# A graph kernel in which each block multiplies the columns up to its own number less two, in place of a number set per strip of four

## Chip, core and metric

The kernel runs on one NeuronCore of a Trainium2 chip. The metric is the device time of one execution in microseconds (us). Before the change the median of four executions is 3410.36 us (3400.29 to 3419.5). The lines of the profile come from one further execution, taken by the hardware profiler.

The engines are named as the profile names them: PE is TensorE's matrix multiply, PEld its weight load, DVE is VectorE, ACT is ScalarE, POOL is GpSimd and SP is SyncE, which here only issues DMAs. "ACTq" and "SPq" are the issuing of DMAs by ACT and SP. An f32 matmul of the program appears in the profile as two MATMUL rows, each with its weight load.

## What is computed

There are 3327 nodes with 128 features (padded to 3328, 26 blocks of 128) and a sparse adjacency matrix `adj` of 3327 x 3327 floats. Two layers follow each other:

```python
h = relu(layernorm(x))                       # layer 0: GATv2, four heads
s = exp(8 * tanh(leaky_relu(x1[:,None] + x2[None,:]) @ a / 8)) * adj
x = x + concat_heads(leaky_relu((s / s.sum(-1)) @ h @ Wlin.T)) @ w
h = relu(layernorm(x))                       # layer 1: GCN
A_t = adj + I;  D = rowsum(A_t) ** -0.5
x = x + relu((D[:,None] * A_t * D[None,:]) @ (h @ W.T + b))
```

The change is in layer 1's product of the adjacency matrix with the new features: (26 blocks of rows) x (26 blocks of columns), each of 128 x 128. "Column j" below is a block of 128 columns of `adj`, and it needs the finished layer-1 features of block j.

## The kernel before, in words

Layer 0 goes over the 26 blocks of rows, one after the other, some 125 us each in the middle of the kernel. For a block, two halves (`hb`) of nine groups (`m`) run: rows of the non-zero neighbours are gathered from a table in DRAM by indirect DMAs (L595, POOL), turned on PE (L622, result `z`), joined with the block's own features on DVE (L638, result `r`), reduced to scores on PE (L657) and summed with their weights (L706, L724). The order on each engine is written out by hand: the main loop calls `slot()`, some 108 times a block, and each slot steps generators on by one `yield`: the rest of a score (`finish`), the close of a block (`close`), and the preparation of the next block (`prep`).

`close(b)` (L729 to L799) ends a block: among others ACT scales the sums (L740), PE turns and multiplies (L746, L757, L768), DVE adds the residual and stores it (L772, L774), ACT centres it (L779, L780, L785), PE multiplies by layer 1's weights (L792), and ACT writes layer 1's features of the block over `x_sb[:, b]` (L797). From then on the block is "closed", and others may multiply with it.

`prep(b)` runs beside the block b - 1. It loads the rows of `adj`, turns them four columns at a time on PE (L365), copies them to SBUF as `at` on ACT (L367) and stores them to DRAM as `AT_d` (L370, issued by ACT). Here layer 1 begins: `known_step` multiplies the columns that are closed (`x_sb[:, j]`) with the transposes while these are still in SBUF. One call, a group, handles up to four columns: an accumulating matmul for each (L379), then a copy (L383, first group) or an addition on DVE (L385) into `part1`, which SP stores at the end (L387). How many columns a block does so is `finished(b)`: 4 * (b // 4) - 2, so 2 for blocks 4 to 7, 6 for 8 to 11, then 10, 14 and 18, and 22 for blocks 24 and 25. In all this makes 244 matmuls in 72 groups.

All that is left is worked off strip by strip, a strip `s` being four blocks of rows, so a matmul (`x_sb[:, j]` against the stored transposes of four blocks) has 512 columns:

- `begin()`: in the last block and a half, strips 1, 2 and 3 do twelve columns each, from `finished(4 * s)` on. SP brings the transposes two columns at a time (`bring`, L913: `adjb<-AT_d`) into a ring of three; the 36 matmuls are L924, one in every four slots.
- `layer1()`: the end. 74 pairs (s, j) stand in a list `work`, cut into seven pieces of eleven. `strip()` brings a piece with DMAs that are issued in turn by SP and ACT (L898: `g<-AT_d`) into one of the four gather buffers. The matmuls are L988; the first of them are put between the last slots of block 25. At a strip's end `strip_out` adds the parts of before (loaded by `strip_in`, L943 to L947), turns, scales and stores the result (L955 to L968).

`columns()` makes the DMAs of a part: consecutive columns of a strip, up to four, are one DMA for each block of rows. The pieces that matter below are the fifth and sixth: the fifth holds strip 2's columns 24 and 25, strip 3's 22 to 25 and strip 4's 14 to 18; the sixth strip 4's 19 to 25 and strip 5's 18 to 21. The seventh has the rest of strip 5 and strip 6 (blocks 24 and 25). Before the change, the DMAs of the fifth to seventh piece are 16, 12 and 6.

Of the kernel before, what the change touches and what calls it, by code (L numbers as in the profile page):

```python
# [15 lines left out]
P = 128  # L16
# [215 lines left out]
def _sparse_layers(tc, nc, x, adj, w1, w2, a, wlin, w, gw, gb, gb_sb, gwT, x_sb, dinv, flag, ident, out):  # L232
# [15 lines left out]
    NB = NP // P  # L248
# [8 lines left out]
    with ExitStack() as l0:  # L257
# [70 lines left out]
        def bank():  # L328
            return ps_tr.tile([P, 4, P], F32, name="tr").rearrange("p a b -> p (a b)")
# [14 lines left out]

        def finished(b):

            return max(0, 4 * (b // 4) - 2)

        def load(b):
            blks[b].adjb = pa.tile([P, NP], F32, name="adjb")  # L350
# [2 lines left out]
        def prep(b, k):  # L353
# [7 lines left out]
            def tables_step(j0):  # L361
                n = min(4, NB - j0)
                pt = ps_tr.tile([P, 4, P], F32, name="tr")
                for q in range(n):
                    nc.tensor.transpose(pt[:, q, :], adjb[:, (j0 + q) * P:(j0 + q + 1) * P], ident)  # L365
                at = pat.tile([P, 4, P], F32, name="at") if b else blks[0].at[j0 // 4 % 4]
                nc.scalar.copy(at[:, :n, :], pt[:, :n, :])  # L367
                at0 = b * TURN + j0 * P * P
                eng = nc.scalar if b else nc.sync
                eng.dma_start(AT_d[at0:at0 + n * P * P].rearrange("(b p c) -> p b c", p=P, c=P), at[:, :n, :])  # L370
                js = range(min(n, finished(b) - j0))
                if len(js):
                    known.append(known_step(j0, js, at))
# [471 lines left out]
        def allow(kind):  # L845
            state[kind] += 1
# [27 lines left out]
        PAIR = 2  # L874
        BEGUN = 12
        strips = {}
        early = {s: range(finished(4 * s), finished(4 * s) + BEGUN) for s in (1, 2, 3) if finished(4 * s) + BEGUN < NB - 3}

        def columns(v, part):

            at = 0
            while at < len(part):
                s, j = part[at]
                n = 1
                while n < 4 and at + n < len(part) and part[at + n] == (s, j + n):
                    n += 1
                for b in range(4 * s, min(4 * s + 4, NB)):
                    a0 = b * TURN + j * P * P
                    c0 = (b - 4 * s) * P
                    yield v[:, at:at + n, c0:c0 + P], AT_d[a0:a0 + n * P * P].rearrange("(j p i) -> p j i", p=P, i=P)  # L890
                at += n

        def strip(part):
            g = rows_in()
            v = g.rearrange("p t c -> p (t c)")[:, :PIECE * 4 * P].rearrange("p (j i) -> p j i", j=PIECE)
            for k, (to, of) in enumerate(columns(v, part)):
                eng = nc.scalar if k % 2 else nc.sync
                eng.dma_start(to, of)  # L898
            for at, key in enumerate(part):
                strips[key] = v[:, at]  # L900

        def begin():

            work = [(s, j) for s in early for j in early[s]]
            pairs = [work[i:i + PAIR] for i in range(0, len(work), PAIR)]
            if not work:
                return
            thirds = pa.tile([P, NP], F32, name="adjb")[:, :3 * PAIR * BANK].rearrange("p (k j i) -> p k j i", k=3, j=PAIR)

            def bring(k):  # L910
                if k < len(pairs):
                    for to, of in columns(thirds[:, k % 3], pairs[k]):
                        nc.sync.dma_start(to, of)  # L913

            for k in range(3):
                bring(k)
            for _ in range(14):
                yield
            po = None
            for i, (s, j) in enumerate(work):  # L920
                assert blks[j].closed
                if j == early[s][0]:
                    po = bank()
                nc.tensor.matmul(po, x_sb[:, j, :], thirds[:, i // PAIR % 3, i % PAIR], start=(j == early[s][0]), stop=(j == early[s][-1]))  # L924
                if i % PAIR == PAIR - 1:
                    bring(i // PAIR + 3)
                if j == early[s][-1]:
                    part2 = pv.tile([P, H, P], F32, name="outT").rearrange("p h i -> p (h i)")
                    nc.scalar.copy(part2, po)
                    nc.sync.dma_start(part2_d[:, 4 * s * P:4 * s * P + BANK], part2)  # L930
                for _ in range(4):
                    yield

        def first_column(s):
            return early[s][-1] + 1 if s in early else finished(4 * s)

        def strip_in(s):

            n = min(4, NB - 4 * s)
            r0 = pr.tile([P, 2, BANK], F32, name="r0", bufs=3).rearrange("p k (b d) -> p k b d", b=4)[:, :, :n]  # L940
            r1 = pr.tile([P, 2, BANK], F32, name="r1").rearrange("p k (b d) -> p k b d", b=4)[:, :, :n]
            rows = slice(4 * s * P, (4 * s + n) * P)
            nc.sync.dma_start(r0[:, 0], xn_d[rows, :].rearrange("(b p) d -> p b d", p=P))  # L943
            if finished(4 * s):
                nc.sync.dma_start(r1[:, 0], part1_d[:, rows].rearrange("p (b i) -> p b i", b=n))
            if s in early:
                nc.sync.dma_start(r0[:, 1], part2_d[:, rows].rearrange("p (b i) -> p b i", b=n))  # L947
            return n, rows, r0, r1

        def strip_out(s, po, n, rows, r0, r1):  # L950

            ot, t, xo = r0[:, 1], r1[:, 1], r0[:, 0]
            po = po[:, :n * P].rearrange("p (b i) -> p b i", b=n)
            if s in early:
                nc.vector.tensor_add(ot, po, ot)  # L955
            if finished(4 * s):
                nc.vector.tensor_add(ot, ot if s in early else po, r1[:, 0])
            elif s not in early:
                nc.scalar.copy(ot, po)
            yield  # L960
            yield
            pt = ps_tr.tile([P, 4, P], F32, name="tr")
            for k in range(n):
                nc.tensor.transpose(pt[:, k, :], ot[:, k, :], ident)
            nc.vector.tensor_add(t, pt[:, :n, :], x_sb[:, 4 * s:4 * s + n, :])
            nc.vector.tensor_tensor(t, t, dinv[:, 4 * s:4 * s + n, None].to_broadcast([P, n, D]), OP.mult)
            nc.vector.scalar_tensor_tensor(xo, t, 0.0, xo, op0=OP.max, op1=OP.add)
            nc.scalar.dma_start(out[rows, :].rearrange("(b p) d -> p b d", p=P), xo)  # L968
# [8 lines left out]
        def layer1():  # L977
            ending, sums, ins = [], {}, {}
            for i, (s, j) in enumerate(work):
                if i == in_front:  # L980
                    yield "all"
                w = min(4, NB - 4 * s) * P
                if s not in sums:
                    sums[s] = ps_z.tile([P, 2, BANK], F32, name="z")[:, 0]
                if j == min(NB - 1, first_column(s) + 4 * (s not in front)):
                    assert len(ending) < 2
                    ins[s] = strip_in(s)
                nc.tensor.matmul(sums[s][:, :w], x_sb[:, j, :], strips[s, j][:, :w], start=(j == first_column(s)), stop=(j == NB - 1))  # L988
                if i % PIECE == PIECE - 1 or i == len(work) - 1:
                    allow("g")  # L990
                ending[:] = [f for f in ending if next(f, "end") != "end"]
                if j == NB - 1:
                    ending.append(strip_out(s, sums.pop(s), *ins.pop(s)))
                yield "one"
            for e in ending:
                for _ in e:
                    pass
# [194 lines left out]
        with tc.manual_schedule():  # L1192
# [4 lines left out]
            n = len(groups)  # L1197
# [8 lines left out]
            for i in range(-1, n + 1):  # L1206
                if i + 1 < n:
                    slot()
                if 0 <= i < n:
                    b, hb, m = groups[i]  # L1210
                    if (b, hb, m) == (max(0, NB - 2), 1, 0):
                        state["early"] = begin()
                    rs[i] = stage_z(blks[b], hb, m, slot, partial(scores, i - 1))
                elif i == n:
                    scores(i - 1)
            lay = layer1()
            todo = "one"
            while ends or tails or state["early"] is not None:
# [67 lines left out]
def kernel(  # L1286
# [26 lines left out]
    gb_sb = const.tile([P, D], F32, name="gb_sb")  # L1313

    _sparse_layers(tc, nc, x, adj, w1, w2, a, wlin, w, gw, gb, gb_sb, gwT, x_sb, dinv, flag, ident, out)


# [46 lines left out]
```

## Time and profile before

| what | value |
|---|---|
| median of four executions | 3410.36 us (3400.29 to 3419.5) |
| the profiled execution, its own time | 3408.4 us |
| its span, first to last instruction | 3406.7 us |
| mean granted TensorE clock | 0.886 |
| DMA traffic | 826.94 MB, mean 243 GB/s |
| busy: POOL 1711.0 us (50%), ACT 685.0 us (20%) | |
| last slot of block 25 to the end | about 3310 us to 3406.7 us |

The page of the profile gives busy times and shares of the span, a strip of 40 slices, DMA queues, the chain of work that ended last, and the costliest groups of instructions. A group's line names the source line, the engine, the operation, what is written and read, the number of instructions, then its busy time, the mean nanoseconds of one, and the idle time of the engine just before it with what ended most of that. A PE row's duration includes its way through the array, so rows that follow each other overlap; the spacing of starts tells what one of them costs.

### The profile page before, as it was taken

What the parts mean: (1) busy time and instruction counts of PE and PEld (TensorE: products, weight loads), DVE (VectorE), ACT (ScalarE), POOL (GpSimd) and SP (SyncE); (2) the same over time, 40 slices, a digit from 0 to 9 for tenths busy, and PEclk for the clock granted to TensorE, in tenths of its full rate; (3) what the DMA queues carried; (4) which work ended last, traced back from release to release, by engine and by line L of the source; (5) the groups of instructions that cost most, each with busy time, mean ns of one, the idle gap of its engine ahead of it and who ended that gap; (6) DMA issues with size and microseconds to landing.
All of it is one profiled execution on the core that took longest, in us unless ns stands there. A gap on an engine that the chain in (4) does not pass through costs nothing.

```text
span 3406.7 us, 52385 instructions
## 1 busy us (share of the span) xinstructions
PE 2634.4 (77%) x19410; PEld 1840.0 (54%) x19410; DVE 2097.5 (62%) x6426; ACT 685.0 (20%) x1703; POOL 1711.0 (50%) x1822
## 2 busy tenths in 40 slices
PE   6687777877787787787777877777777787777887
PEld 4464555555464565565555555555555565555553
DVE  6676666666666666665665665665665665665442
ACT  3122122212211221221121221221221221121110
POOL 3555555555554545545545555545545445445420
PEclk8789888899988988888988898988898988888999
DMA  9978777777777867867867777777776777777886
GB/s 327 316 258 264 220 250 260 222 253 260 254 237 238 265 213 251 263 199 241 272 204 238 255 227 228 251 229 225 250 241 217 249 235 221 242 217 218 259 256 185
DMA packets 417844, 826.94 MB, mean 243 GB/s; under 512 B 38435, under 2 KB 288815, under 8 KB 414255
## 3 DMA queue, kind: packets, MB, share of 16 engines
q0 software_dynamic: 141440, 619.41, 55.6%
q1 hardware_dynamic: 165343, 147.87, 14.0%
q10 hardware_dynamic: 110800, 56.25, 5.6%
q8 instruction: 156, 2.56, 0.3%
q14 instruction: 105, 0.86, 0.1%
HBM read 754.47 MB, written 113.22 MB: 255 GB/s over the span
## 4 chain that ended last, share of the span: by engine, by line
PE 52%; DVE 17%; issue 12%; another core or an unknown queue 10%; DMA 5%; POOL 2%; ACT 1%; SPq 0%; ACTq 0%; DVEq 0%; POOLq 0%
PE z L622 19%; PE s L657 10%; DVE r L638 9%; PE ag L706 5%; PE z L627 3%; PE tr L675 3%; POOL g L595 2%; DVE cand L422 2%; PE tr L379 2%; PE ag L724 2%; DMA g<-table,idx 1%; DMA g<-AT_d 1%; PE z L988 1%; PE tr L365 1%
## 5 line engine op out<-in xcount | busy, mean ns | idle before, releaser
L595 POOL DMA_INDIRECT g<-table,idx x1664 | 1588.7, 955 | 1363.7 <-PE ag L706 800.2
L638 DVE TENSOR_TENSOR r<-z,x1n 128x1024 f32<-128x1024 f32 x832 | 1011.7, 1216 | 844.2 <-remote 318.8
L622 PE MATMUL z<-ident,g 128*128 128x128 f32 x6656 | 1051.1, 303 | 167.2 <-issue 109.1
L622 PEld LDWEIGHTS z<-ident,g 128*128 128x128 f32 x6656 | 857.0, 157 | 352.5 <-issue 232.4
L657 PE MATMUL s<-r,sel 128*2 128x512 f32 (+1 forms) x3744 | 549.1, 606 | 132.5 <-DVE r L638 82.8
L666 ACT COPY ssb<-s 128x512 f32<-128x512 f32 x260 | 147.1, 566 | 842.2 <-PE s L657 275.8
L706 PE MATMUL ag<-g,wt 128*32 128x133 f32 x3328 | 234.8, 309 | 99.1 <-issue 97.9
L657 PEld LDWEIGHTS s<-r,sel 128*2 128x2 f32 x3744 | 82.6, 84 | 404.4 <-issue 271.3
L675 PE MATMUL tr<-ident,ssb 128*128 128x128 f32 x988 | 172.3, 300 | 105.1 <-issue 97.3
L706 PEld LDWEIGHTS ag<-g,wt 128*32 128x32 f32 x3328 | 134.4, 118 | 219.4 <-issue 210.3
L422 DVE MAX8 cand<-codes 128x8 f32<-128x52 uint16 x1664 | 216.2, 201 | 0.0
L675 PEld LDWEIGHTS tr<-ident,ssb 128*128 128x128 f32 x988 | 129.5, 155 | 131.5 <-issue 115.6
L595 POOL DMA_INDIRECT ge<-table,idxo x104 | 99.1, 953 | 180.5 <-PE ag L724 90.2
L379 PE MATMUL tr<-at,x_sb 128*128 128x128 f32 x488 | 96.4, 353 | 115.3 <-ACT at L367 109.7
L367 ACT COPY at<-tr 128x512 f32<-128x512 f32 (+1 forms) x175 | 97.4, 557 | 416.0 <-remote 199.4
L686 ACT ACTIVATE th<-sc 128x32 f32<-128x32 f32 x260 | 58.8, 226 | 506.5 <-DVE sc L681 235.8
L379 PEld LDWEIGHTS tr<-at,x_sb 128*128 128x128 f32 x488 | 81.0, 249 | 141.7 <-ACT at L367 130.5
L633 DVE TENSOR_TENSOR r<-z,x1n 128x128 f32<-128x128 f32 x104 | 30.2, 290 | 195.4 <-PE z L627 147.0
L365 PE MATMUL tr<-ident,adjb 128*128 128x128 f32 x676 | 123.2, 308 | 33.7 <-DMA adjb<-in_adj_dram 15.6
L627 PE MATMUL z<-oi,x1b 128*128 128x256 f32 x416 | 137.3, 414 | 4.9 <-issue 4.9
L453 DVE MAX8 lists<-cand 128x8 f32<-128x272 f32 (+1 forms) x338 | 133.0, 394 | 2.2
L622 PE MATMUL z<-ident,ge 128*128 128x128 f32 x416 | 89.2, 291 | 45.5 <-issue 33.2
(199 smaller groups left out, 2614.3 us busy)
## 6 DMA issues: line engine op xcount, KB each, us to landing
adjb<-in_adj_dram SPq DMA_DIRECT2D x26, 1664.0 KB
table<-AT_d SPq DMA_DIRECT2D x26, 1664.0 KB
AT_d<-at ACTq DMA_DIRECT2D x150, 256.0 KB
g<-table,idx POOLq DMA_INDIRECT x1664
table<-img SPq DMA_DIRECT2D x12, 1296.0 KB
adjb<-AT_d SPq DMA_DIRECT2D x72, 128.0 KB
g<-AT_d SPq DMA_DIRECT2D x25, 256.0 KB
g<-AT_d ACTq DMA_DIRECT2D x25, 256.0 KB
```

Of the source, the lines that this page charges most:

```text
L365: nc.tensor.transpose(pt[:, q, :], adjb[:, (j0 + q) * P:(j0 + q + 1) * P], ident)
L379: nc.tensor.matmul(pq[:, :P], x_sb[:, j0 + q, :], at[:, q, :], start=(q == 0), stop=(q == js[-1]))
L422: nc.vector.max(cand[:, c, 8:].rearrange("p (r s) -> p r s", s=32)[:, :, sgm % 32], codes.rearrange("p a b -> p (a b)")[:, sgm % 32 * SEG: ...
L453: nc.vector.max(top, of)
L595: return nc.gpsimd.indirect_dma_start(out=g[:, t, lo:hi], out_offset=None, in_=tab, in_offset=bass.IndirectOffsetOnAxis(ap=at[:, t:t + 1], ...
L622: nc.tensor.matmul(z[:, i, q * P:(q + 1) * P], g[:, m % 2 * 4 + q, c0:c0 + D], ident, is_transpose=True, start=(q == 0 or m < 8), stop=(m ...
L627: nc.tensor.matmul(z[:, i, :n], k.x1b[:, h * D:(h + 1) * D], k.oi[:, hb * n:(hb + 1) * n], start=False, stop=True, skip_group_check=True)
L638: nc.vector.tensor_tensor(r.rearrange("p h (i s) -> p h i s", s=16), z.rearrange("p h (i s) -> p h i s", s=16), k.x1n[:, 2 * hp:2 * hp + 2 ...
L657: nc.tensor.matmul(k.s[32 * h:32 * h + 2, :n], sel[:, h, 31 - at:33 - at], r[h // 2][:, h % 2, :n], start=(at == 0), stop=(at == 1 or m == 8))
L666: nc.scalar.copy(ssb[:, :nk * P], s[:, :nk * P])
L675: nc.tensor.transpose(pt[:, q, :], ssb[:, q * P:(q + 1) * P], ident)
L706: nc.tensor.matmul(ag[32 * cg:32 * cg + 32, u, :WORK], wt[:, t].rearrange("p h q -> p (h q)"), g[:, t, f0:f0 + WORK], start=(w == 0 and t ...
```

## The change

`finished(b)` becomes b - 2 for every block from 4 on. So block 5 multiplies three columns beside its transposes, block 6 four, block 7 five, and so on. What begins a strip in `begin()` and `layer1()` is still `finished(4 * s)`, which has the value of before; but a column of which some blocks of the strip already have the product is now brought and multiplied only for the others (`blocks(s, j)` of them), with a narrower matmul. `columns()` joins only columns with the same number of blocks to one DMA.

```diff
         def finished(b):
-            return max(0, 4 * (b // 4) - 2)
+            return b - 2 if b >= 4 else 0
...
+        def blocks(s, j):
+            return sum(finished(b) <= j for b in range(4 * s, min(4 * s + 4, NB)))
...
-                while n < 4 and at + n < len(part) and part[at + n] == (s, j + n):
+                while n < 4 and at + n < len(part) and part[at + n] == (s, j + n) and blocks(s, j + n) == blocks(s, j):
                     n += 1
-                for b in range(4 * s, min(4 * s + 4, NB)):
+                for b in range(4 * s, 4 * s + blocks(s, j)):
...
-                nc.tensor.matmul(po, x_sb[:, j, :], thirds[:, i // PAIR % 3, i % PAIR], start=(j == early[s][0]), stop=(j == early[s][-1]))
+                w = blocks(s, j) * P
+                nc.tensor.matmul(po[:, :w], x_sb[:, j, :], thirds[:, i // PAIR % 3, i % PAIR, :w], start=(j == early[s][0]),
+                                 stop=(j == early[s][-1]), skip_group_check=True)
...
-                w = min(4, NB - 4 * s) * P
+                w = blocks(s, j) * P
...
-                nc.tensor.matmul(sums[s][:, :w], x_sb[:, j, :], strips[s, j][:, :w], start=(j == first_column(s)), stop=(j == NB - 1))
+                nc.tensor.matmul(sums[s][:, :w], x_sb[:, j, :], strips[s, j][:, :w], start=(j == first_column(s)), stop=(j == NB - 1),
+                                 skip_group_check=True)
```

Counted on the two built programs, the change moves this:

| line before | before | after |
|---|---|---|
| L379 matmul of 128 columns | 244 | 275 |
| L385 addition on DVE (a group after a block's first) | 50 | 55 |
| L924 matmuls of 128 / 256 / 384 / 512 columns | 0 / 0 / 0 / 36 | 3 / 3 / 3 / 27 |
| L988 matmuls of 128 / 256 / 384 / 512 columns | 0 / 4 / 0 / 70 | 3 / 5 / 2 / 64 |
| L913 DMAs | 72 | 78 |
| L898 DMAs on SP, and as many on ACT but for one | 45 and 45 | 50 and 49 |

## Prediction

> **What bounds the kernel now.** I began with the totals and the chain of work that ended last. No engine is full: PE 77%, DVE 62%, but half of the chain is PE's own work. I then went to the group that grows, L379 (the products beside the transposes), and asked for its line alone.
>
> ```profile
> span 3406.7 us, 52385 instructions
> PE 2634.4 (77%) x19410; PEld 1840.0 (54%) x19410; DVE 2097.5 (62%) x6426; ACT 685.0 (20%) x1703; POOL 1711.0 (50%) x1822
> ...
> PE 52%; DVE 17%; issue 12%; another core or an unknown queue 10%; DMA 5%; POOL 2%; ACT 1%; SPq 0%; ACTq 0%; DVEq 0%; POOLq 0%
> PE z L622 19%; PE s L657 10%; DVE r L638 9%; PE ag L706 5%; PE z L627 3%; PE tr L675 3%; POOL g L595 2%; DVE cand L422 2%; PE tr L379 2%; PE ag L724 2%; DMA g<-table,idx 1%; DMA g<-AT_d 1%; PE z L988 1%; PE tr L365 1%
> ...
> L379 PE MATMUL tr<-at,x_sb 128*128 128x128 f32 x488 | 96.4, 353 | 115.3 <-ACT at L367 109.7
> ```
>
> To see: L379 is 488 rows for 244 matmuls, 96.4 us of PE, so 0.395 us a matmul; its 115.3 us of idle time before it is more than its work, nearly all waiting for ACT's copy L367 of the transposes. In the trace, 38 of its 72 groups start with under half a microsecond of PE idle, 34 with 1 to 6 us, most near 3; 115.3 / 34 is 3.4 us for such a one.
>
> Whether that work is on the path is told by the kernel itself, since blocks differ in it. ACT's row sum of `adj` (L443) comes once in each preparation; the timeline of ACT has its starts. These are those of blocks 3, 7, 11, 15, 19, 23 and 25:
>
> ```profile
> 315.07 2.96 ACT L443 ACTIVATE adjb<-adjb 128x3328 f32<-128x3328 f32 x1
> ...
> 795.96 2.96 ACT L443 ACTIVATE adjb<-adjb 128x3328 f32<-128x3328 f32 x1
> ...
> 1281.02 2.96 ACT L443 ACTIVATE adjb<-adjb 128x3328 f32<-128x3328 f32 x1
> ...
> 1778.75 2.96 ACT L443 ACTIVATE adjb<-adjb 128x3328 f32<-128x3328 f32 x1
> ...
> 2281.77 2.96 ACT L443 ACTIVATE adjb<-adjb 128x3328 f32<-128x3328 f32 x1
> ...
> 2786.85 2.96 ACT L443 ACTIVATE adjb<-adjb 128x3328 f32<-128x3328 f32 x1
> ...
> 3042.31 2.96 ACT L443 ACTIVATE adjb<-adjb 128x3328 f32<-128x3328 f32 x1
> ```
>
> The first column is the start. Divided by the blocks between them, a block takes 120.2, 121.3, 124.4, 125.8, 126.3 and 127.7 us, with 2, 6, 10, 14, 18 and 22 matmuls in it. Blocks with more of them are longer.
>
> Last, the timeline of ACT in the end, where layer 1's loads are issued (columns: start, duration, what; in brackets the idle time before and what ended it):
>
> ```profile
> 3321.49 18.14 ACTq L898 DMA_DIRECT2D g<-AT_d  x18
> 3339.67 0.63 ACT L740 ACTIVATE agn<-ag,rec 128x128 f32<-128x128 f32 x2 [24.50 <-DMA g<-AT_d]
> ...
> 3345.99 8.00 ACTq L898 DMA_DIRECT2D g<-AT_d  x6
> 3354.10 0.40 ACT L779 ACTIVATE agn<-xn,st 128x128 f32<-128x128 f32 x1 [7.52 <-DMA g<-AT_d]
> ```
>
> To see: the close of block 25 (L740, L779) stands behind loads in ACT's order, and ACT is held by issuing them, 18.14 us and 8.00 us. PE's timeline shows PE idle 6.86 us before L746, which L740 releases, and 0.81 us before L784, which L779 releases. Between those PE is busy.
>
> **The change part by part.** All against the profiled execution's 3408.4 us, 2.0 us under the median of the runs shown.
>
> *1. 31 matmuls more at L379, in 5 more groups.* Blocks with b mod 4 = 1, 2, 3 get one, two, three more in each of the strips of blocks 4 to 23, and block 25 one: 5 x 6 + 1 = 31. A fifth column opens a new group only where b mod 4 = 3: five groups, each with a DVE addition (0.28 us by the line's median), a PSUM buffer and a wait for its copy L367. PE's own work: 31 x 0.395 = 12.2 us. What of it lengthens a block comes from the periods: (127.7 - 120.2) / 20 = 0.375 us a matmul, its share of groups in it, so 31 x 0.375 = 11.6 us. But the periods also drift within equal counts, and the later steps are smaller: from 10 to 22 matmuls (127.7 - 124.4) / 12 = 0.275, so 8.5 us. I take 10 us. Bounds: nothing, if the work fills PE's idle 23%; and 12.2 us plus five long waits of 3.4 us, 29.2 us. A gain is excluded: nothing is taken from these blocks.
>
> *2. 18 block columns less at L924, in the last block and a half.* Twelve PE rows of 512 columns start 0.43 us apart, so a full matmul is 0.86 us and a block's share 0.215 us: 18 x 0.215 = 3.9 us of PE. In the chain between 3150 us and the end L924 has 9.7% of 257 us, 24.9 of the 36 x 0.86 = 31.0 us that it works, or 0.8. So -3.1 us, between 0 and -3.9. Six more DMAs on SP (78 for 72, 1.2 MB less in all) are hidden by the ring: a pair is brought three pairs ahead, some 28 us, and the rows of L913 take about half a microsecond to issue. The SP loads queued behind them (L587, L774) keep their places between the same brings. If the cover went, PE would wait for a pair's landing, as in the chain's pieces `DMA adjb<-AT_d` of 4 to 6 us.
>
> *3. 13 block columns less at L988.* 13 x 0.215 = 2.8 us, at PE's busy stretch from 3354 us on, so -2.8 us.
>
> *4. More DMAs for less data in the end.* The fifth piece has 18 for 16, the sixth 18 for 12, the seventh 7 for 6. Where ACT stood for 18 issues before L740 it now stands for 19, and before L779 for 9 in place of 6. An issue waits for an earlier DMA to land (SP's queue: L898 waited 24.2 us in 22 times on `g<-AT_d`; both share eight completion semaphores, so the n-th issue waits for the n-8th). So the cost goes by bytes that must have landed, at 260 GB/s in this stretch: before L740 two single blocks more, 0.13 MB or 0.5 us. In the sixth piece the last issue waited for the 4th DMA (16 blocks of 64 KB) and now waits for the 10th (16 + 12 + 1 + 1 = 30 blocks): 14 x 64 KB, 3.5 us. PE, which already waits 0.81 us there, waits for all of it, with its later matmuls in order behind L784; DVE's and ACT's next steps of the close too. After the 6.86 us idle the granted clock in 3340 to 3344 us was 0.50 and four L988 rows took 3.42 us, not 1.7; I add half of that difference, 0.8 us. Together +4.8 us; bounds 0 (the loads land early, there being 0.8 MB less) and +11 (every issue at the row's mean, 1.01 + 3 x 1.33 = 5 us, the clock's whole 1.7, and SP's four more issues at 1.1 us ahead of the parts that L955 adds).
>
> Sum: +10 - 3.1 - 2.8 + 4.8 = +8.9 us, 3417.3 us for the profiled execution and 3419 us on the median.
>
> One rule of the Trainium skill speaks against the change more strongly. "TensorE: Matmul & The Clock Gate", section "Back-to-back issue gap", gives for a stream of weight loads and matmuls about 81 ns at 128 columns and 131 ns at 512: a block's column alone then costs 2.5 times its share in a strip of four. The rows here say 0.395 against 0.215 us, 1.8 times. By the page part 1 would be 31 x 2.5 x 0.215 = 16.7 us of PE in place of 12.2 us; I stay with the rows.
>
> **The rivals.**
>
> *A. The new groups stall PE in full (slower).* Each of the five new groups (blocks 7, 11, 15, 19, 23) meets the long wait for L367, 3.4 us, and none of the matmuls finds cover: 12.2 + 17.0 - 3.1 + 2.0 = +28.1 us, 3438 us on the median. It decides (over 0.5%, 17 us) from 1.2 us a new group on, with the matmuls uncovered. For it: 34 of 72 groups have such a wait. Against it: from 2 to 22 matmuls five groups are added too, and a block grows only 7.5 us, not 7.9 + 17.
>
> *B. PE's idle time swallows part 1 (a little faster).* Then parts 2 and 3 remain with 0.5 us of part 4: -5.4 us, 3405 us. For it: PE idles 23%, and the first step, 2 to 6 matmuls, cost only 1.1 us a block. Against it: the later blocks.
>
> *C. The end does not get shorter but longer.* The list of 74 pairs stays, the DMAs become more, and ACT holds the close for part 4's upper bound: 10 - 3.1 - 2.8 + 11 = +15 us, 3426 us. So the change would do the opposite of its name in the end. For it: 24.50 and 7.52 us of ACT behind these loads. Against it: 0.8 MB less to bring.
>
> **How the numbers follow.** Forecast 0.62, A 0.16, B 0.12, C 0.10. A measurement of this kernel can tell about 0.5% from no change: 3393 to 3427 us is the same. The forecast and B lie inside; A lies above; of C a third passes the edge with an unlucky part 1. That gives 0.79 the same, 0.19 slower, and 0.02 faster, since all work that leaves the last 300 us is 6.7 us of PE. The range goes from under B to near A: 3402 to 3436 us.
>
> **What would show it.** L379 with 550 rows and about 108 us busy; periods of the blocks with b mod 4 = 3 up by a microsecond or more, of b mod 4 = 0 unchanged; L740 late by about half a microsecond against block 25's last L724 and L779 by 4 us; PE idle before L784 up from 0.81 to some 4 us; the stretch from L784 to the end shorter by 2.8 us. I am wrong if the periods do not grow, or if the new groups' waits at L367 show more than 3 us each on top of them.

## The result, and the profile after

The changed kernel takes 3421.97 us (median of 52 executions, 3401.57 to 3441.94), the kernel before, run beside it, 3408.84 us (78 executions, 3386.67 to 3426.55). The ratio is 1.0042 with a 95% interval from 1.0032 to 1.0053, so the change costs 14.3 us, between 10.9 and 18.1: clear of no change, and under the half percent. The forecast was 3419 us, +8.9 us.

Single executions scatter by 40 us, three times the effect. The profiled execution of the changed kernel happens to be a short one; its span is that of before to the tenth. So its total says nothing, and only stretches inside it are read, beside the same stretches of other kernels where these were profiled. First its page, totals and L379:

```profile
span 3406.7 us, 52541 instructions
PE 2624.2 (77%) x19472; PEld 1852.7 (54%) x19472; DVE 2099.7 (62%) x6431; ACT 682.4 (20%) x1703; POOL 1710.1 (50%) x1822
...
L379 PE MATMUL tr<-at,x_sb 128*128 128x128 f32 x550 | 112.3, 364 | 116.4 <-ACT at L367 110.9
```

To see: 62 rows more at L379 for the 31 matmuls, 112.3 us busy for 96.4. The idle time before them, 116.4 us, has hardly grown for five groups more. In the trace the first rows of the five new groups (blocks 7, 11, 15, 19 and 23) have 0.0, 2.3, 0.0, 0.5 and 0.0 us of PE idle before them, so only one of them meets a long wait.

The periods between the starts of L443 did not grow in this execution: from block 3 to block 25 it is 2725.5 us, 2727.2 before. By the prediction's own sign ("I am wrong if the periods do not grow") that speaks against it, but one execution cannot carry the sign. The same stretch takes 2737.6 us with the added products alone (the first experiment below) and 2724.4 us without them (the second).

ACT's timeline in the end (L902 is L898 of before):

```profile
3322.97 18.20 ACTq L902 DMA_DIRECT2D g<-AT_d  x19
3341.22 0.62 ACT L740 ACTIVATE agn<-ag,rec 128x128 f32<-128x128 f32 x2 [24.87 <-DMA g<-AT_d]
...
3347.54 8.42 ACTq L902 DMA_DIRECT2D g<-AT_d  x9
3356.06 0.40 ACT L779 ACTIVATE agn<-xn,st 128x128 f32<-128x128 f32 x1 [7.94 <-DMA g<-AT_d]
```

To see: 19 issues took 18.20 us where 18 took 18.14, and nine took 8.42 us where six took 8.00. PE's timeline says the same (columns: start, duration, engine and line, what, number; in brackets the idle time before):

```profile
3356.51 0.34 PE L784 MATMUL tr<-ident,agn 128*128 128x128 f32 x1 [1.11 <-ACT agn L779]
3356.69 4.46 PE L994 MATMUL z<-g,x_sb 128*128 128x512 f32 x10
```

PE waits 1.11 us there, not 4. From block 25's last L724 to the last instruction the kernel before took 79.8 us and this one takes 78.3 us: 12.8 us to L740 (12.7 before), 14.8 to L779 (14.4), 50.6 to the end (52.6). In this pair the end is 1.5 us shorter; how far that holds in other kernels is said below.

### The profile page after: what moved, and what is told of

It reads as the page before. It is cut to its first block, busy times and chain, and to the rows that moved or that the text cites. A ratio compares the mean times of both kernels' runs of the same rounds, so it can differ in the third digit from the quotient of the medians.

```text
span 3406.7 us, 52541 instructions
## 1 busy us (share of the span) xinstructions
PE 2624.2 (77%) x19472; PEld 1852.7 (54%) x19472; DVE 2099.7 (62%) x6431; ACT 682.4 (20%) x1703; POOL 1710.1 (50%) x1822
## 4 chain that ended last, share of the span: by engine, by line
PE 51%; DVE 18%; another core or an unknown queue 12%; issue 11%; DMA 4%; POOL 2%; ACT 1%; ACTq 0%; SPq 0%; DVEq 0%; POOLq 0%
PE z L622 18%; PE s L657 10%; DVE r L638 9%; PE ag L706 4%; PE z L627 3%; PE tr L675 2%; DVE cand L422 2%; PE tr L379 2%; PE ag L724 2%; POOL g L595 2%; DMA g<-table,idx 1%; DVE codes L410 1%; PE z L994 1%; PE tr L365 1%
## 5 line engine op out<-in xcount | busy, mean ns | idle before, releaser
L622 PE MATMUL z<-ident,g 128*128 128x128 f32 x6656 | 1061.8, 304 | 179.5 <-issue 130.7
L622 PEld LDWEIGHTS z<-ident,g 128*128 128x128 f32 x6656 | 866.5, 158 | 354.8 <-issue 246.5
L657 PE MATMUL s<-r,sel 128*2 128x512 f32 (+1 forms) x3744 | 537.6, 599 | 149.8 <-DVE r L638 99.4
L657 PEld LDWEIGHTS s<-r,sel 128*2 128x2 f32 x3744 | 81.5, 83 | 412.1 <-issue 266.1
L379 PE MATMUL tr<-at,x_sb 128*128 128x128 f32 x550 | 112.3, 364 | 116.4 <-ACT at L367 110.9
L675 PEld LDWEIGHTS tr<-ident,ssb 128*128 128x128 f32 x988 | 126.1, 152 | 127.7 <-issue 111.8
L367 ACT COPY at<-tr 128x512 f32<-128x512 f32 (+1 forms) x175 | 97.2, 555 | 421.8 <-remote 233.7
L379 PEld LDWEIGHTS tr<-at,x_sb 128*128 128x128 f32 x550 | 95.6, 260 | 145.2 <-ACT at L367 133.5
L627 PE MATMUL z<-oi,x1b 128*128 128x256 f32 x416 | 129.9, 395 | 1.1 <-issue 1.1
```

The source lines that it names most:

```text
L379: nc.tensor.matmul(pq[:, :P], x_sb[:, j0 + q, :], at[:, q, :], start=(q == 0), stop=(q == js[-1]))
L622: nc.tensor.matmul(z[:, i, q * P:(q + 1) * P], g[:, m % 2 * 4 + q, c0:c0 + D], ident, is_transpose=True, start=(q == 0 or m < 8), stop=(m ...
L627: nc.tensor.matmul(z[:, i, :n], k.x1b[:, h * D:(h + 1) * D], k.oi[:, hb * n:(hb + 1) * n], start=False, stop=True, skip_group_check=True)
L657: nc.tensor.matmul(k.s[32 * h:32 * h + 2, :n], sel[:, h, 31 - at:33 - at], r[h // 2][:, h % 2, :n], start=(at == 0), stop=(at == 1 or m == 8))
L675: nc.tensor.transpose(pt[:, q, :], ssb[:, q * P:(q + 1) * P], ident)
```

## The experiments

There were twelve runs. A ratio is against the kernel before on the same chip, and comes with its 95% interval; it is not the quotient of the two medians, and where these say something else, it is told. The chips were not alike: on most of them the kernel before takes about 3400 us, on one it took 2500 us; where that matters it is said.

Theory M is the prediction's: the added matmuls cost by their number. Theory E: the blocks hide them and the end loses. After the first runs came theory G: the groups cost, not the matmuls in them.

**The blocks alone.**

```diff
+        def beside(b):
+            return b - 2 if b >= 4 else 0
...
-                js = range(min(n, finished(b) - j0))
+                js = range(min(n, beside(b) - j0))
...
-                if j0 + len(js) == finished(b):
+                if j0 + len(js) == beside(b):
```

> Part 1 of the change alone: 31 matmuls more in 5 more groups at L379 of the kernel before; the early strips and the end stay as before, so the 31 products are counted twice in the output. Theory M (the matmuls in the blocks cost, the rest nearly cancels): +10 us over before, between +8 and +14. Theory E (the blocks hide them, the loss is in the last 300 us, where DMAs became more): within 3 us of before.

Ratio 1.0063 (1.0036 to 1.0091), +21 us, between 12 and 31; the medians, 3420.19 and 3405.37 us, differ by 14.8 us. Against E; M's +8 to +14 touches the interval at its lower end.

**The rest alone**: the changed kernel, with `beside(b)` as `max(0, 4 * (b // 4) - 2)` at these two places.

> Parts 2 to 4 alone: the blocks multiply 244 columns as before, but the early strips and the end leave the 31 block columns out, so these are missing from the output. Theory M: -1 us against before, between -5 and +3. Theory E: +10 us or more.

Ratio 1.0018 (0.9998 to 1.0038), +6 us, between -1 and +13. M's -1 us is at the edge of the interval, E's 10 us is inside. The medians, 3401.90 and 3405.37 us, differ by 3.5 us the other way, so the size of this part is not settled. In its profile the stretch after L724 is 78.8 us.

**The added columns without the new groups.**

```diff
-            return b - 2 if b >= 4 else 0
+            return min(b - 2, 4 * (b // 4)) if b >= 4 else 0
```

> finished(b) is min(b - 2, 4 * (b // 4)): 26 matmuls more at L379 than before, none of them in a new group, and the early strips and the end cover the rest. Theory M (cost by the matmul, 0.3 to 0.4 us each): 26 / 31 of the change's loss, +9 to +12 us. Theory G (the five new groups, each with its wait for ACT's copy, are most of the loss): within 4 us of before.

Ratio 1.0017 (0.9993 to 1.0041), +6 us, between -2 and +14. The medians differ by 0.9 us. Neither M's 9 to 12 us nor G's 4 us is excluded; the middle of the interval, for 26 of the 31 matmuls, is less than half of the change's 14.3 us.

**The added products four times.**

```diff
-                for q in js:
-                    nc.tensor.matmul(pq[:, :P], x_sb[:, j0 + q, :], at[:, q, :], start=(q == 0), stop=(q == js[-1]))
+                qs = [q for q in js for _ in range(4 if j0 + q >= 4 * (b // 4) - 2 else 1)]
+                for i, q in enumerate(qs):
+                    nc.tensor.matmul(pq[:, :P], x_sb[:, j0 + q, :], at[:, q, :], start=(i == 0), stop=(i == len(qs) - 1))
```

> The changed kernel, with each of the 31 added products multiplied four times over in its group (the output has them four times): 93 matmuls more than the change, no more groups. Theory M: +28 to +37 us over the change, 0.3 to 0.395 us a matmul. If PE's idle time takes such work: under +15 us. Theory G: also under +15 us.

Ratio 1.0075 (1.0050 to 1.0099), +26 us over before, so 11 us over the change for 93 matmuls: 0.12 us each, with the two intervals together between 0.02 and 0.22. M's 0.3 to 0.395 falls. Both other theories said under 15 us, and stand.

**One group more in 22 blocks**, in the kernel before:

```diff
-                js = range(min(n, finished(b) - j0))
+                more = b >= 4 and j0 == -(-finished(b) // 4) * 4
+                js = range(1 if more else min(n, finished(b) - j0))
...
-                    nc.tensor.matmul(pq[:, :P], x_sb[:, j0 + q, :], at[:, q, :], start=(q == 0), stop=(q == js[-1]))
+                    nc.tensor.matmul(pq[:, :P], x_sb[:, j0 + q if j0 + q < finished(b) else 0, :], at[:, q, :], start=(q == 0), stop=(q == js[-1]))
...
-                if j0 + len(js) == finished(b):
+                if j0 + len(js) > finished(b):
```

> The kernel before, with one group more in each of blocks 4 to 25: the next four transposes after the last group get one matmul with column 0 of the features (so the output has 22 products too many). 22 matmuls and 22 groups more. Theory G (a group costs, not its matmuls): 2 us or more for each, +40 to +60 us over before. Theory M: 22 x 0.3 to 0.4, +7 to +9 us.

This and the next three shared a chip on which the kernel before takes 2499.64 us. There the ratio is 1.0008 (0.9995 to 1.0022): 22 groups cost at most 6 us. It told nothing of the chips of the prediction, so it was run again:

> one_more_group again (22 groups and 22 matmuls more, 22 products too many in the output), because that run's chip executed the kernel before in 2500 us, not 3405 us. On a chip where the kernel before takes about 3400 us: theory G (a new group costs 1.5 to 2 us, its matmuls little) +35 to +47 us; theory M (0.3 to 0.4 us a matmul, groups for nothing) +7 to +9 us. On a chip of the other kind: within 5 us, as before.

Where the kernel before takes 3398.87 us the ratio is 1.0058 (1.0031 to 1.0085), +20 us, between 11 and 29, or 0.9 us for a group with its matmul: above M's 9 us and under G's 35. Neither theory had it right.

**The same with a later start**: a `yield` ahead of `pq = bank()` in `known_step`, so that ACT's copy has more time.

> As one_more_group (22 products too many), but every group starts one step of the preparation later, so that ACT's copy L367 should be done when PE comes to it. If a group costs by PE's wait for this copy (G, wait): at least two thirds of the loss of one_more_group are gone. If it costs by its PSUM buffer and its addition on DVE (G, buffer): the loss stays within 5 us of one_more_group's.

Ratio 1.0119 (1.0092 to 1.0147), a loss of 30 us, on the chip of 2500 us, where the groups cost at most 6 us and there was no loss to take away.

**The later start in the kernel before.**

> The kernel before, with every group started one step of the preparation later, all results as before. G, wait: the 72 groups' idle time at L367 (115 us) mostly goes, and 20 to 60 us of it leave the span. If that idle time only moves to the next wait: within 8 us of before.

Ratio 1.0058 (1.0035 to 1.0081) on that chip: a loss of 14 us, outside both expectations. PE's idle time before L379 is 0.0 us in this profile and 0.6 us in the run before it, where the kernel with one group more had 40.7 us on the same chip; both kernels became longer all the same. So a wait that is gone is not time won here. Whether a later start helps where L379 waits long for the copy is untested.

**All of the end's loads on SP**, in the changed kernel:

```diff
-                eng = nc.scalar if k % 2 else nc.sync
-                eng.dma_start(to, of)
+                nc.sync.dma_start(to, of)
```

> The changed kernel, with all 99 loads of the end issued by SP, so that ACT's part of the close of block 25 (L740, L779) stands behind none. If ACT's issues hold the end (part 4 of the prediction): L740 some 15 us earlier and the time 4 to 10 us under the change's. If the end waits for the data anyway: within 3 us of the change, or above it.

Ratio to the kernel before 0.9934 (0.9910 to 0.9958), -16.5 us on the chip of 2500 us; the change alone did not run there. ACT's timeline:

```profile
2412.19 0.63 ACT L740 ACTIVATE agn<-ag,rec 128x128 f32<-128x128 f32 x2 [11.79 <-DVE rec L735]
...
2425.73 0.40 ACT L779 ACTIVATE agn<-xn,st 128x128 f32<-128x128 f32 x1 [4.32 <-DVE st L773]
```

To see: L740 now follows DVE at once, 0.5 us after the start of the last L724, where the other three profiles of this chip have 11 to 14 us. From L779 to the end it is 60.9 us instead of some 52, so most of that is given back: from the last L724 to the end it is 74.9 us, 78.1 in the kernel with one group more. The larger gain lies ahead of the last L724. The loads of the earlier pieces stand in ACT's order too, between the scores of block 25. ACT's timeline of the kernel before has it:

```profile
3280.36 6.82 ACTq L898 DMA_DIRECT2D g<-AT_d  x6
3287.23 0.23 ACT L686 ACTIVATE th<-sc 128x32 f32<-128x32 f32 x1 [6.78 <-DMA g<-AT_d]
```

There are three such bursts of six issues, of 6.82, 7.10 and 6.82 us. With all loads on SP they are gone from ACT, and from block 25's L443 to its last L724 it is 205.4 us, where the other three profiles of this chip, with the wide early strips of before, have 214.2, 213.7 and 215.4 us. The narrower strips are forecast to save 3 us of that. The prediction saw ACT's issues as a hold on the close alone.

**The best of both**: no new groups, and the end on SP.

> no_new_group (finished(b) = min(b - 2, 4 * (b // 4))) with all loads of the end issued by SP. If ACT's issues hold the end: 8 to 15 us under no_new_group, so 4 to 12 us faster than before. If not: as no_new_group, 0 to +6 us against before.

Ratio 0.9982 (0.9954 to 1.0009) where the kernel before takes 3398.87 us: -6 us by the ratio, not told from no change; the ratios of the two kernels differ by some 12 us, the medians' differences by 4, and the intervals overlap. From the last L724 to the end 73.4 us, 6 us under the kernel before, but only 1.5 us under the profile of the added columns without the new groups (74.9 us), in which L740 happens to come early, 9.0 us after the last L724. From block 25's L443 to its last L724 it is 273.2 us for 277.7. What comes late next is seen on PE's timeline (here L962 and L969 are L957 and L964 of before):

```profile
3369.30 1.11 PE L969 MATMUL tr<-ident,r 128*128 128x128 f32 x4 [3.40 <-DVE r L962]
3370.20 9.59 PE L993 MATMUL z<-g,x_sb 128*128 128x512 f32 x16
```

SP's loads of the parts now stand behind the 50 loads, and DVE's addition of them waits 7.3 us for their landing (`DMA r<-part_d`). After the 3.40 us idle 16 matmul rows took 9.59 us; the same sixteen took 7.03 us before.

**Every group.** As one group more, with `j0 >= finished(b)` in place of `j0 == ...`, and the store after the last:

> As one_more_group, but every four transposes without a group get one, with one matmul of column 0: 82 groups and 82 matmuls more than before (82 products too many in the output). On a chip where the kernel before takes about 3400 us: by one_more_group_2 (20 us for 22, 0.9 us each) +75 us over before, between +40 and +110. If groups cost nothing but their matmuls at 0.12 us (the slope of added_four_times): +10 us.

Ratio 1.0155 (1.0124 to 1.0187), +53 us for 82 groups: 0.64 us for a group with its matmul, between 0.5 and 0.8. In its profile the blocks show it: from block 3's L443 to block 25's it is 2789.6 us, 62 us more than in the kernel before.

**The added products twelve times**: 12 in place of 4.

> As added_four_times, each of the 31 added products twelve times over: 341 matmuls more than the change, no more groups. On a chip where the kernel before takes about 3400 us, over before: +27 us + 0 if matmuls were free beyond the change (+14 us); +55 us at 0.12 us each; +142 us at the prediction's 0.375 us each.

Ratio 1.0223 (1.0189 to 1.0257), +76 us, so 62 us over the change for 341 matmuls: 0.18 us each, between 0.14 and 0.22 with both intervals. From block 3's L443 to block 25's it is 2795.7 us, 68 us more than in the kernel before.

## Why the prediction was right, and where it was not

The time lies in the range and on the side forecast, and in the likeliest case, the same within half a percent. The terms of the sum fared differently.

*Part 1, the matmuls beside the transposes: the place right, the prices wrong.* The prediction took 0.395 us as PE's work for one added matmul, from the mean of the line, and 0.375 us as its price, from the periods of the blocks. The line's rows in the runs with four times, with twelve times, and with every group give both anew (L380 is L379 of before):

```profile
L380 PE MATMUL tr<-at,x_sb 128*128 128x128 f32 x736 | 134.9, 345 | 117.3 <-ACT at L367 107.9
...
L380 PE MATMUL tr<-at,x_sb 128*128 128x128 f32 x1232 | 194.0, 321 | 120.7 <-ACT at L367 113.0
...
L379 PE MATMUL tr<-at,x_sb 128*128 128x128 f32 x652 | 140.0, 354 | 135.6 <-ACT at L367 111.0
```

Against the changed kernel's 550 rows and 112.3 us, a matmul more in a running group keeps PE busy 0.24 us by both runs (22.6 us for 93, 81.7 us for 341). The mean of 0.395 us holds, among other things, what a group costs once. So PE's work for the 31 matmuls is 31 x 0.24 = 7.4 us, not 12.2. Of the 0.24 us some 0.18 (0.14 to 0.22) reach the time: PE's idle time takes about a quarter, not all. A new group with one matmul, in the last row against the 488 rows and 96.4 us of before, keeps PE busy 0.53 us and adds 0.25 us of idle time before its rows; 0.64 us reach the time, so 0.64 - 0.18, some 0.5 us, are the group's own. The kernel with a group at every four transposes shows what the periods had meant. Its L443, for blocks 3, 7, 11, 23 and 25:

```profile
316.61 2.96 ACT L443 ACTIVATE adjb<-adjb 128x3328 f32<-128x3328 f32 x1
...
817.28 2.96 ACT L443 ACTIVATE adjb<-adjb 128x3328 f32<-128x3328 f32 x1
...
1327.92 2.96 ACT L443 ACTIVATE adjb<-adjb 128x3328 f32<-128x3328 f32 x1
...
2849.61 2.96 ACT L443 ACTIVATE adjb<-adjb 128x3328 f32<-128x3328 f32 x1
...
3106.19 2.96 ACT L443 ACTIVATE adjb<-adjb 128x3328 f32<-128x3328 f32 x1
```

A block takes 125.2 us at the start, 127.7 us next, 126.3 to 127.1 us after that and 128.3 us at the end, where the kernel before went from 120.2 over 121.3 to 127.7. All blocks have seven groups here, with 8 matmuls in the first four and 23 in the last two. The growth has shrunk from 7.5 to 3.1 us, for 15 matmuls, which is 0.2 us each; what made the early blocks short before was, by this, their one group. These are single executions (the kernels with no or few added products have 118 to 123 us for the first four), so the sizes are rough. In the kernel before groups and matmuls grow together, so its periods could give only their common price. The change adds 31 matmuls with 5 groups, where the periods had 20 with 5. At the two prices it is 31 x 0.18 + 5 x 0.5 = 8.1 us, between 6 and 10 with their intervals. That is near the 10 us taken, but composed otherwise, so this nearness is luck.

*Part 2, the early strips: not contradicted, not shown.* From block 25's L443 to its last L724 four profiled kernels with the change's early strips take 286.0, 280.3, 279.1 and 281.2 us (mean 281.6), four with full ones 284.6, 284.6, 283.5 and 283.1 (mean 284.0): -2.4 us, forecast -3.1. One of the four speaks against it, and the four scatter by 7 us, so -2.4 us is not told from nothing.

*Part 3, the narrower matmuls of the end: right where it can be read.* From L779 to the end 50.6 us for 52.6: -2.0 us, forecast -2.8 with 0.8 us of slow clock against it. Three more profiles with the narrower matmuls have 50.9, 50.7 and 52.9 us, three more with full ones 52.4 each; the 52.9 us (the added products four times) speaks against it.

*Part 4, ACT's issues in the end: the size failed.* The step said that the sixth piece's last issue must wait for 14 blocks more at 260 GB/s, 3.5 us. From L740 to L779 it became 0.4 us longer. The wait itself was placed rightly: in the traces the last issue waits on the semaphore of the 4th DMA before and of the 10th after. But the step counted the DMAs ahead by their place in the list, and they do not land in that order, since SP issues its half ahead of ACT. In the kernel before the 4th DMA, issued by ACT at 3346.41 us, landed at 3353.6; by then the 5th, 7th and 9th, issued by SP between 3345.24 and 3346.32 us, had landed too, at 3349.6, 3351.8 and 3353.3 us. That makes 26 blocks landed, not 16. In the changed kernel it is 31 when the 10th lands, at 3355.3 us. So five blocks more, 1.3 us at 260 GB/s, were to be waited for, not 14; that only 0.4 us is seen is one pair of executions. Four profiles each give a mean of 14.2 us from L740 to L779 with the end of before and 14.8 us with the change's.

The issues before L740 were to cost 0.5 us. L740 comes 12.8 us after the last L724 (12.7 before), but over the other profiled kernels of 3400 us with loads on both engines it is 9.0 to 13.6 us, so that term cannot be read.

*The rivals.* A let each of the five new groups meet a wait of 3.4 us; their five waits are 2.8 us together in the changed kernel. It needed 1.2 us for a new group to decide; it is some 0.5 us. B had the cover, but only a quarter of the added work finds it, and the blocks alone cost 12 us at the least. C let the end grow by some 8 us after the last L724 (11 us in its part 4 against 2.8 us saved). The profiles do not show that: with the change's end it takes 78.3, 78.8, 81.5 and 77.9 us, with the end of before 79.8, 78.3, 79.4 and 80.2 us. That is no difference in either direction. The total of the rest alone, -1 to +13 us, would still allow C.

*What stays open.* Parts 1 to 4 at their measured sizes give 8.1 - 2.4 - 1.5 = about +4 us; the change measures 14.3 us, at least 10.9. The blocks alone measured 21 us, at least 12 (14.8 us by the medians), where the two prices give 8.1 us, at most 10. So some of the blocks' part, 2 us at the least by the ratio, is not explained by counting matmuls and groups. Whether it belongs to where the five groups stand in their blocks was not tested. Nor was the clock: in the executions of the changed kernel on record a granted clock lower by 0.001 goes with some 1.6 us more, and the blocks alone had 0.884 on average, the kernel before on the same chip 0.886, a difference within its noise. That the forecast came within 6 us is thus partly luck: part 1 lacks something, and part 4 was too large by some 4 us, which made up for it.

On the page of the Trainium skill cited in the prediction ("TensorE: Matmul & The Clock Gate", "Back-to-back issue gap"): its ratio of 2.5 would have given more PE work, an estimated 16.7 us. The prediction answered with 0.395 against 0.215 us, 1.8 times, but that sets a mean busy time against a spacing of starts. Inside a group the rows of L379 start 0.112 us apart where the granted clock is full, two to a matmul, so 0.224 us against 0.215 us, 1.04 times. At half clock both double nearly: rows start 0.213 us apart, and rows of 512 columns 0.854 us where it was 0.43. The rows of this case, all f32, show neither 1.8 nor 2.5, and the measurement decides.

## What to carry to other kernels

A slope read from a kernel's own blocks is the price of everything that grows with them; ask what else grew (here the groups), and make one run that changes one without the other before the slope is used. Nor is a line's mean the price of one more: here the mean was 0.395 us, and one more took 0.24 us of PE and 0.18 us of time. Where two engines issue DMAs in turn, look in the trace at what has landed when a wait ends before counting what stands ahead in the list. When single executions scatter by more than the effect, multiply the suspected cost until it stands out, and read totals only from many executions.

## What the runs showed of the hardware

The kernel before takes about 3400 us on most chips here and 2500 us on one, with the same instructions. The page of the run with one group more on the latter:

```profile
span 2497.6 us, 52507 instructions
PE 2253.6 (90%) x19454; PEld 1599.7 (64%) x19454; DVE 2067.4 (83%) x6448; ACT 682.0 (27%) x1703; POOL 1738.9 (70%) x1822
...
PEclk8699999999999999999999999999999999999999
```

The granted clock is 0.979 there, 0.876 to 0.889 in the profiled executions on the others; it was at half for 104 us instead of 774 us of the kernel before's span. DVE and POOL are busy for nearly the same time (2067.4 and 1738.9 us, 2097.5 and 1711.0 in the kernel before), but many waits are gone: the idle time put down to ACT's copy before PE's L379 is 15 us with 94 groups, where the kernel before has 240 us with 72 (both PE and its weight loads counted). In the kernel before 39 of ACT's 175 copies L367 start over 4 us after the recorded end of the transposes that they copy; in this run 2 of 175 do. What holds the kernel back on the others was not tried. A price measured on one such chip did not hold on the other: 22 groups cost 20 us (11 to 29) where the kernel before takes 3400 us and at most 6 us where it takes 2500 us.
